# A list schedule's allowance for attention work on VectorE: fixed at 1.5, or 0.2 and 2.0 by the attention's share of the steps

## The chip, the cores and the metric

The kernel runs on one core of a Trainium2 chip. The time is the device time of one execution in microseconds (us). The profile is of one execution, taken by the hardware profiler. Engines: PE is TensorE's matmul row and PEld its weight loads, DVE is VectorE, ACT is ScalarE, POOL is GpSimd, SP is SyncE, which issues the DMAs.

## What is computed

The input x is 8 images of 56 x 56 places with 256 channels. Layer 0 is a group norm, a routed window attention with a depthwise 3 x 3 convolution, an output projection and a residual. Layer 1 takes the result as 3136 tokens per image: a layer norm, an attention over a window of 7 neighbours with a residual, then a layer norm and a recurrence over the tokens with a residual. In outline:

```python
# layer 0, for each of 49 regions of 64 places, 8 heads
score, index = top_k(q @ gathered_keys, 32)   # of 256 keys
out = softmax(score) @ v[index]
x = x + (out + conv3x3(v)) @ out_w + out_b
# layer 1
t = t + local_attention(layer_norm(t))        # 3 tokens to each side
# recurrence, batch 8, 3136 steps
i, o = sigmoid(x_t @ U + b + h @ V) ; g = tanh(...)
c = h * c + i * g
h = o * tanh(c)
t = t + hs
```

The recurrence is serial: each step needs the h of the step before it. The forget gate of the source is computed but not used, so three gates remain.

## The kernel before

The images are cut into 7 rows of 448 tokens. A unit is one row of one image; there are 56 units, row by row, the 8 images within a row. A unit takes queries and the convolution, then 7 regions. For each region, two pairs of head groups get scores from TensorE, and VectorE finds the top 32 of 256 by rounds of MAX8 and MATCH_REPLACE8 (each MATCH_REPLACE8 comes with a small MATCH_VALUE_LOAD). ScalarE takes exponentials, TensorE transposes and multiplies with the values. Behind a unit come its output projection, the local attention of layer 1 and the gates' input terms (tile gs), which go to DRAM (xgd) and are loaded again for the recurrence (r_gin). All of this is called attention here.

A step of the recurrence runs over four engines: 48 matmuls add h times the gate weights to the input terms (r_sum), ScalarE takes a tanh (r_th), VectorE transposes it (STREAM_TRANSPOSE r_cell<-r_th), VectorE scans to the new cell (TENSOR_TENSOR_SCAN r_c), ScalarE takes a second tanh (r_tc), and VectorE multiplies to the new h (SCALAR_TENSOR_TENSOR r_hs). This order is the chain. Beside it GpSimd prepares the next cell's product (r_cell<-r_hs,r_half). A row's steps can begin once that row is through attention in all 8 images. So the first steps stand beside the second row, and the last 451 steps can only follow the last attention. These last steps take the output gate's sum in a bank of its own, which leaves less on the chain.

The order of the instructions on each engine is made by the class _Plan. Every operation is first recorded with two estimates in ns: held, for which its engine is taken, and late, after which its result can be used (function _time). Operations of the recurrence's chain have chain set. _Plan.run then goes through time event by event. For each free engine it takes the first ready operation in order of rank, which is mostly the recurrence before attention, then the order of recording. An operation that isn't of the chain is held back if it would end after a bound called until. The function expected (line 414) gives due, the time at which the chain will next need the engine, by adding up late and a hop of 70 ns between engines. The bound is due plus an allowance. For the engines other than VectorE the allowance is a constant (SLACK, line 63: 60 for PE, ACT and POOL). For VectorE it is 1.5 times the time left until due, at least 20 (line 445). Where PE has nothing for more than 220 ns, a filler matmul on tile spare is put in (FILL). The estimates only make the order; on the chip each instruction waits for its semaphores. All recorded instructions have the helper's line 308 in the profile, the fillers line 661.

At the end of _layers, the loop over the units records attention and, at each row's second image, the steps whose row is complete (follow, line 1464). After the loop the remaining steps are recorded, and nc.run makes the order.

Of the kernel before, what the change touches and what calls it, by code (L numbers as in the profile page):

```python
# [56 lines left out]

HOP = 70
FAR = 10**12
FILL = 220  # L60
LONG = 400
CLEAR = 250
SLACK = {"PE": 60, "DVE": 120, "ACT": 60, "POOL": 60, "SP": 1000}
# [176 lines left out]
class _Plan:  # L240
# [137 lines left out]
    def run(self, tc, fill):  # L378
        ops = self.ops
        for tag in self.tags.values():  # L380
            for i, buf in enumerate(tag):
                kin = [b for b in tag[:i] if b.stream == buf.stream][-1:] if buf.free else tag[i - 1 : i]
                before = [(b.users[0], 0) for b in kin]
                if i >= buf.bufs and not buf.free:
                    before += [(u, None) for u in tag[i - buf.bufs].users]
                for u, gap in before:
                    for v in buf.users:
                        if u is not v:
                            g = gap
                            if g is None:  # L390
                                g = u.held if u.engine == v.engine else u.late + HOP
                            u.before[v] = max(g, u.before.get(v, 0))
        for op in ops:
            op.open, op.due = 0, 0
        for op in ops:
            for b in op.before:
                b.open += 1
        engines = ("PE", "DVE", "ACT", "POOL", "SP")
        free = dict.fromkeys(engines, 0)
        later = {e: [] for e in engines}  # L400
        ready = {e: [] for e in engines}
        chain = [o for o in ops if o.chain]
        at, made, events = 0, {}, []

        def opened(op):
            heappush(later[op.engine], (op.due, op.rank, op))
            heappush(events, op.due)

        for op in ops:
            if not op.open:  # L410
                opened(op)
        done, now = [], 0

        def expected(engine):


            t = None
            for k in range(at, min(at + 7, len(chain))):
                op = chain[k]
                if t is None:  # L420
                    if op.open:
                        break
                    t = max(op.due, now)
                else:
                    p = chain[k - 1]
                    t += p.late + (HOP if p.engine != op.engine else 30)
                if op.engine == engine or engine == "POOL" and op.pair:
                    return t - (CLEAR if engine == "POOL" else 0)
            return FAR

        filled = tied = 0
        locked = {"DVE": 0, "POOL": 0}
        since, closed = 0, None
        while len(done) < len(ops) + filled:
            moved = False
            for e in engines:
                if free[e] > now:
                    continue
                while later[e] and later[e][0][0] <= now:
                    _, rank, op = heappop(later[e])  # L440
                    insort(ready[e], (rank, op))
                if not ready[e]:
                    continue
                due = expected(e)
                until = due + (SLACK[e] if e != 'DVE' else max(20, 1.5 * (due - now)))
                for i, (rank, op) in enumerate(ready[e]):
                    if not op.chain and now + op.held > until:
                        continue
                    if op.pair and locked["POOL" if e == "DVE" else "DVE"] > now:
                        continue  # L450
                    if e == "POOL" and op.pair and op.held > LONG and 0 < at < len(chain):
                        if since > 3:
                            continue
                        op.behind = closed
                    if any(b.free and not self._room(b, made, now) for b in op.takes):
                        continue
                    del ready[e][i]
                    op.start = now
                    free[e] = now + op.held
                    if op.pair:  # L460
                        locked[e] = now + op.late
                        heappush(events, locked[e])
                    heappush(events, free[e])
                    heappush(events, now + op.late + HOP)
                    done.append(op)
                    for b in op.takes:
                        if b.free:
                            made.setdefault(id(b.tag), []).append(b)
                    for b, gap in op.before.items():
                        b.due = max(b.due, now + gap)  # L470
                        b.open -= 1
                        if not b.open:
                            opened(b)
                    if op.chain:
                        at += 1
                        since += 1
                        if op.closes:
                            since, closed = 0, op
                    elif e == "POOL" and op.rank[0] == 0:
                        tied += 1  # L480
                    moved = True
                    break
            if not moved and free["PE"] <= now:

                due = min([expected("PE")] + [op[0] for op in later["PE"][:1]])
                if FILL < due - now < FAR // 2:
                    op = _Op()
                    op.trace, op.start = [fill], now
                    filled += 1
                    done.append(op)  # L490
                    free["PE"] = now + FILL
                    heappush(events, free["PE"])
                    moved = True
            if not moved:
                while events and events[0] <= now:
                    heappop(events)
                if not events:
                    raise RuntimeError("the plan has stopped")
                now = heappop(events)
        self.length = now  # L500
        with tc.manual_schedule():
            for op in done:
                for t in op.trace:
                    t()
# [25 lines left out]
def _layers(ctx: ExitStack, tc, a, out):  # L530
# [9 lines left out]
    nc = tc.nc  # L540
# [7 lines left out]
    work = ctx.enter_context(tc.tile_pool(name="work", bufs=3))  # L548
# [89 lines left out]
    for t in cells:  # L638

        nc.vector.memset(t, 0.0)  # L640
        for at in (0, CELL + 2):
            e = t[:, at : at + CELL].rearrange("p (n e) -> p n e", e=3)
# [23 lines left out]
    raw, nc = nc, _Plan(tc)  # L666
    images_p, rowp, keep = nc.pool(images_p, nb), nc.pool(rowp, 2), nc.pool(keep, 2)
    one, work, two = nc.pool(one, 1), nc.pool(work, 3), nc.pool(two, 2)
# [789 lines left out]
    def after(g):  # L1458

        b, unit = units[g]  # L1460
        im, row = images[b], state_of[g]
        return project(b, unit, im, row) + window_attention(b, unit, im, row)

    def follow(first, end):

        with nc.rank(0):
            for k in range(first, end):
                for s in recurrence(k):
                    s()
# [26 lines left out]
            todo = todo[n:]  # L1496
    for s in after(len(units) - 1):
        s()
    made["tokens"] = SHIFTED
    follow(ready, -(-SHIFTED // TB))  # L1500
    nc.run(tc, fill)
# [2 lines left out]
def _body(tc, a, out):  # L1504
    _layers(tc, a, out)
# [64 lines left out]
```

## Time and profile before

| what | us |
|---|---|
| median of 3 runs | 9194.27 (9193.11 to 9199.71) |
| profiled execution, device time | 9180.4 |
| profiled execution, span from first to last instruction | 9178.5 |
| first scan of the recurrence starts | 1339.9 |
| last attention instruction on VectorE starts | 8032.4 |
| last scan starts | 9172.7 |

| engine | busy us | share of the span |
|---|---|---|
| PE | 8792.1 | 96% |
| PEld | 6037.0 | 66% |
| DVE | 7559.4 | 82% |
| ACT | 5939.4 | 65% |
| POOL | 3221.5 | 35% |

PE's share includes the fillers (14904 matmul records, 2072.2 us). The profile's rows of groups give busy time and mean duration of one instruction; instructions of one engine overlap, so that the distance from start to start is shorter than the duration. In the page's row of slices each digit is the busy share of a fortieth of the span, in tenths. A line of waits names who waited, for whom, us in total, times, and the longest. Where this text counts steps, it counts the scans, one per step (3136).

### The profile page before, as it was taken

Reading aid. Unit: us, or ns where it says so; the run is one execution under the profiler, and the core shown is the slowest. Engines: PE = TensorE matmul, PEld = TensorE weight load, DVE = VectorE, ACT = ScalarE, POOL = GpSimd, SP = SyncE. Lnnn points to the kernel's source line nnn. Section 1 sums busy time; section 2 is a strip of 40 time slices with the busy share of each in tenths; the row PEclk is TensorE's granted clock in tenths of the full one; section 3 lists DMA queues with packets and bytes.
Section 4 is the critical chain, followed back from the end, with each engine's and each line's share of the span. In section 5 each row is a group of like instructions: output and inputs, shape, how many; then the busy total and the mean of one; then the engine's idle time right before and its main releaser. Section 6 shows DMA issues by size and latency. Waiting matters only on the chain.

```text
span 9178.5 us, 500794 instructions
## 1 busy us (share of the span) xinstructions
PE 8792.1 (96%) x203918; PEld 6037.0 (66%) x203918; DVE 7559.4 (82%) x32392; ACT 5939.4 (65%) x23551; POOL 3221.5 (35%) x7747
## 2 busy tenths in 40 slices
PE   7999999999999999999999999999999999999999
PEld 4555556666666666666666666666666666688888
DVE  5776799999999899999899999899999999734443
ACT  4665667776666677676676676677766766534444
POOL 1232344444343343343344443434434444311111
PEclk9999999999999999999999999999999999999999
DMA  6545433333332333333333333233333232210000
GB/s 198 155 129 163 111 106 82 93 92 80 93 91 78 91 84 90 89 85 91 88 82 92 91 82 90 78 93 88 83 92 89 80 90 78 60 28 23 23 24 21
DMA packets 1071271, 798.40 MB, mean 87 GB/s; under 512 B 402366, under 2 KB 1001524, under 8 KB 1068964
## 3 DMA queue, kind: packets, MB, share of 16 engines
q1 hardware_dynamic: 1068964, 766.36, 30.8%
q8 instruction: 1604, 26.28, 1.2%
q14 instruction: 703, 5.76, 0.2%
HBM read 527.08 MB, written 238.88 MB: 83 GB/s over the span
## 4 chain that ended last, share of the span: by engine, by line
PE 52%; DVE 25%; ACT 6%; issue 2%; DMA 1%; SPq 0%; POOL 0%; ACTq 0%; DVEq 0%; POOLq 0%
PE r_sum L308 19%; PE mm L308 15%; PE spare L661 12%; DVE left L308 8%; DVE top L308 6%; DVE r_c L308 3%; PE pt_av L308 3%; PE sc L308 3%; DVE r_cell L308 2%; DVE r_hs L308 2%; ACT pe L308 1%; ACT r_th L308 1%; ACT xln L308 1%; DVE st L308 1%; ACT r_sum L308 1%
## 5 line engine op out<-in xcount | busy, mean ns | idle before, releaser
L308 PE MATMUL r_sum<-r_v,r_hs 128*16 128x64 f32 (+2 forms) x150528 | 2758.0, 220 | 160.4 <-DVE r_hs L308 107.1
L308 PEld LDWEIGHTS r_sum<-r_v,r_hs 128*8 128x8 f32 (+2 forms) x150528 | 2224.2, 96 | 907.8 <-DVE r_hs L308 802.6
L308 POOL TENSOR_TENSOR r_cell<-r_hs,r_half 128x16 f32<-128x16 f32 x3136 | 706.7, 225 | 4012.7 <-DVE r_hs L308 3192.8
L661 PE MATMUL spare<-ident 128*32 128x128 f32 x14904 | 2072.2, 276 | 6.2 <-issue 4.5
L308 DVE MATCH_REPLACE8 left<-top,left 128x256 f32<-128x256 f32 x4704 | 1903.3, 408 | 0.0
L308 DVE MAX8 top<-left 128x8 f32<-128x256 f32 x4704 | 1848.2, 413 | 1.8 <-POOL r_cell L308 0.3
L308 ACT ACTIVATE r_th<-r_sum 128x64 f32<-128x64 f32 x3587 | 802.3, 224 | 1559.4 <-PE r_sum L308 1507.1
L661 PEld LDWEIGHTS spare<-ident 128*32 128x32 f32 x14904 | 1474.8, 110 | 309.6 <-issue 263.4
L308 DVE STREAM_TRANSPOSE r_cell<-r_th 128x64 f32<-128x64 f32 x3136 | 812.8, 259 | 882.5 <-ACT r_th L308 842.2
L308 POOL TENSOR_TENSOR pe<-pe,left 128x256 f32<-128x256 f32 x1568 | 1136.2, 729 | 821.5 <-ACT left L308 397.9
L308 ACT ACTIVATE r_tc<-r_c 128x16 f32<-128x16 f32 x3136 | 696.9, 222 | 717.4 <-DVE r_c L308 696.0
L308 DVE TENSOR_TENSOR_SCAN r_c<-r_cell 128x48 f32<-128x48 f32 x3136 | 910.8, 290 | 86.9
L308 ACT ACTIVATE pe<-sc,nmax 128x256 f32<-128x256 f32 x1568 | 710.9, 470 | 185.5 <-DVE left L308 105.3
L308 ACT ACTIVATE left<-left,nmax 128x256 f32<-128x256 f32 x1568 | 773.8, 502 | 13.8 <-DVE left L308 7.8
L308 PE MATMUL pt_av<-ident,pe 128*128 128x128 f32 x3136 | 691.2, 289 | 49.4 <-ACT pts L308 19.4
L308 PE MATMUL mm<-wu,xlT 128*112 128x256 f32 (+3 forms) x1856 | 732.6, 512 | 2.6 <-ACT xlT L308 1.7
L308 DVE MAX8 top<-sc 128x8 f32<-128x256 f32 x1568 | 620.4, 416 | 80.8 <-PE sc L308 80.4
L308 ACT ACTIVATE r_half<-r_c 128x16 f32<-128x16 f32 x3136 | 655.3, 209 | 0.0
L308 DVE SCALAR_TENSOR_TENSOR r_hs<-r_cell,r_tc 128x16 f32<-128x16 f32 x2685 | 545.4, 203 | 124.5 <-ACT r_tc L308 103.4
L308 DVE MATCH_REPLACE8 left<-top,sc 128x256 f32<-128x256 f32 x1568 | 641.2, 412 | 0.7 <-issue 0.6
L308 ACT COPY pts<-pt_av 128x256 f32<-128x256 f32 x1568 | 574.8, 367 | 97.6 <-PE pt_av L308 89.5
L308 PEld LDWEIGHTS pt_av<-ident,pe 128*128 128x128 f32 x3136 | 375.3, 143 | 349.2 <-issue 190.0
(131 smaller groups left out, 12151.6 us busy)
## 6 DMA issues: line engine op xcount, KB each, us to landing
kg<-kd SPq DMA_DIRECT2D x1568, 64.0 KB
vg<-vd SPq DMA_DIRECT2D x1568, 64.0 KB
vshift<-lines SPq DMA_DIRECT2D x336, 232.0 KB
xgd<-gs SPq DMA_DIRECT2D x224, 336.0 KB
r_gin<-xgd SPq DMA_DIRECT2D x1568, 48.0 KB
xchunk<-xt SPq DMA_DIRECT2D x112, 448.0 KB
lines<-v SPq DMA_DIRECT2D x112, 290.0 KB
xn<-xh SPq DMA_DIRECT2D x56, 560.0 KB
```

Source lines behind the costliest of these rows:

```text
L308: made[:] = [method(*[v.real() if isinstance(v, _View) else v for v in args], **{k: v.real() if isinstance(v, _View) else v for k, v in kw ...
L661: raw.tensor.matmul(spare[:32, :P], ident[:, :32], ident, start=True, stop=True, skip_group_check=True)
```

## The change

The factor 1.5 for VectorE is replaced by a function, yields. It keeps account of spent, the estimated VectorE time (held) of all operations placed so far that are not of the chain. work is the sum of held over all such operations recorded before the last 451 steps (nc.last marks that place), and beside is the number of chain operations there. begun is what was spent when the first chain operation was placed, and at is the number of chain operations placed. Attention counts as ahead when what was spent since begun is more than the share at / beside, plus AHEAD = 0.02, of what was left at begun. Then the factor is 0.2; otherwise it is 2.0. Every other rule of the list stays.

```diff
+AHEAD = 0.02
...
+        beside = sum(o.chain for o in ops[:self.last])
+        work = sum(o.held for o in ops[:self.last] if o.engine == "DVE" and not o.chain)
+        begun = 0
+
+        def yields():
+
+            ahead = spent - begun - (at / beside + AHEAD) * (work - begun)
+            return 0.2 if ahead > 0 else 2.0
+
-        filled = tied = 0
+        filled = tied = spent = 0
...
-                until = due + (SLACK[e] if e != 'DVE' else max(20, 1.5 * (due - now)))
+                until = due + (SLACK[e] if e != "DVE" else max(20, yields() * (due - now)))
...
+                    if e == "DVE" and not op.chain:
+                        spent += op.held
                     if op.chain:
+                        begun = begun if at else spent
                         at += 1
...
+        self.spent = spent
...
+    nc.last = len(nc.ops)
     made["tokens"] = SHIFTED
     follow(ready, -(-SHIFTED // TB))
     nc.run(tc, fill)
```

## The prediction

> **What bounds the kernel now.** I read the page first, then busy time by stage, then the recurrence's scans counted by stage, then VectorE's waits and a stretch of its timeline.
>
> From the page:
>
> ```profile
> span 9178.5 us, 500794 instructions
> ...
> DVE  5776799999999899999899999899999999734443
> ...
> PEclk9999999999999999999999999999999999999999
> ...
> PE 52%; DVE 25%; ACT 6%; issue 2%; DMA 1%; SPq 0%; POOL 0%; ACTq 0%; DVEq 0%; POOLq 0%
> ```
>
> VectorE (DVE) is nearly full from slice 7 to slice 34, where attention runs beside the recurrence, and at 40% once the attention is done. TensorE's clock is full throughout. Busy time by stage (columns: length; busy time and instructions of PE, PEld, DVE, ACT, POOL; clock; DMA):
>
> ```profile
> 1340.00:4000.00 2660.00, 2568.42 (x65014) 1725.24 (x65011) 2466.90 (x10618) 1856.49 (x7484) 1074.22 (x2565) 1.00 0.33 88
> 4000.00:7700.00 3700.00, 3571.05 (x90567) 2387.54 (x90569) 3413.91 (x14693) 2574.66 (x10384) 1492.97 (x3581) 1.00 0.33 87
> ```
>
> The same for the instructions on tile r_c alone; VectorE's count there is the number of scans, one per step:
>
> ```profile
> 1340.00:7700.00 6360.00, 743.93 (x2471) 830.85 (x4942) 1.00 0.33 87
> ...
> 8032.00:8220.00 188.00, 22.21 (x83) 27.86 (x166) 1.00 0.11 29
> 8220.00:9178.00 958.00, 106.26 (x449) 150.34 (x899) 1.00 0.08 23
> ```
>
> This decides the reading. A step takes 6360/2471 = 2.574 us beside attention, 188/83 = 2.265 us in the same form once VectorE has no attention left (its last such instruction starts at 8032.4), and 958/449 = 2.13 us in the late form that splits off the output gate. VectorE carries about five attention operations, near 1.7 us by their start distances, in a step that is only 0.31 us longer for them. So **the chain of the recurrence sets the time, not the amount of VectorE work**: the attention ends early, and 451 late steps follow whatever happens. What counts is by how much each attention operation delays the chain.
>
> I then split the 2.574 us by the starts in the trace (means over the first 2560 steps, against the usual value where nothing interferes): scan to second tanh 0.376 (0.293), that tanh to the h product 0.271 (0.256), product to first matmul 0.325 (0.235), first tanh to transpose 0.314 (0.256), transpose to scan 0.296 (0.296). VectorE's own share is the last two and the second: 148 us from a late transpose, 39 us from a late product, nothing between transpose and scan. ScalarE and TensorE cost more. VectorE's waits over 1340 to 7700 agree: it waits for the chain in only 350 of 2470 transposes, otherwise it comes to it from attention work.
>
> ```profile
> DVE r_cell L308 <- ACT r_th L308: 241.5, 350, 3.6
> DVE r_hs L308 <- ACT r_tc L308: 69.2, 216, 3.0
> ```
>
> VectorE's timeline (start, duration, instruction):
>
> ```profile
> 3108.29 0.41 DVE L308 MAX8 top<-left 128x8 f32<-128x256 f32 x1
> 3108.63 0.40 DVE L308 BATCH_NORM_STATS2 st<-t 112x6 f32<-112x256 f32 x1
> ...
> 3111.70 0.27 DVE L308 STREAM_TRANSPOSE r_cell<-r_th 128x64 f32<-128x64 f32 x1
> 3111.87 0.25 DVE L308 SCALAR_TENSOR_TENSOR r_res<-mm,r_res 128x128 f32<-128x128 f32 x1
> 3112.05 0.24 DVE L308 TENSOR_TENSOR_SCAN r_c<-r_cell 128x48 f32<-128x48 f32 x1
> ...
> 3114.15 0.26 DVE L308 STREAM_TRANSPOSE r_cell<-r_th 128x64 f32<-128x64 f32 x1
> 3114.45 0.26 DVE L308 TENSOR_TENSOR_SCAN r_c<-r_cell 128x48 f32<-128x48 f32 x1
> ```
>
> Independent instructions overlap: what follows a MAX8 starts 0.34 us after it (median 0.341), though it is busy for 0.41; what follows the transpose starts 0.165 to 0.17 after it. The scan needs the transpose's result and starts 0.296 after it (last two lines). So between the two there is room for about 0.13 us of other work; the r_res operation there already puts the scan at 0.345.
>
> **The change, part by part.** It adds no instruction, DMA or tile. It replaces the factor 1.5 in VectorE's test by 0.2 or 2.0, depending on whether attention is ahead of its share plus 2%. What this does to the list I take from the two built orders of VectorE, counted up to the last match_replace (2565 steps before the change, 2624 after it), by the three gaps that a step has.
>
> *Transpose to scan.* The code's estimates: the transpose holds VectorE for 166 ns, its scan is due at 276, so 110 remain; a MAX8 is put at 326. Factor 1.5 allows 110 + 165 = 275, factor 2.0 allows 110 + 220 = 330. So at 2.0, and not at 1.5, a whole MAX8 passes in front of the scan. The orders show it: operations of 0.33 us and more in this gap go from 0 to 798 (789 of them MAX8). No row of before has one there. By the start distances the scan moves from 0.296 to 0.165 + 0.341 = 0.506, so +0.210 us each: 798 x 0.210 = **+168 us**. Bounds: 0 if other engines are late anyway; without overlap 0.258 + 0.413 - 0.296 = 0.375 each, 299 us. I take 0.210, built from the nearest rows, and correct for other engines below. Against that, operations of about 0.2 us there go from 133 to 57, at 0.05 each: -4 us.
>
> The Trainium skill, page "VectorE: DVE Perf Modes", section "The DRAIN you can't avoid", says that the next operation does not start until the pipe is empty (and that one that is not held starts earlier). Read strictly, that is the 299 us; the rows above show the overlap, so I go by them.
>
> *Product to next transpose.* With factor 0.2 a fourth long operation is mostly refused. I added up the start distances of the operations in this gap (MAX8 0.341, match load plus match_replace 0.399, others likewise), and took the mean from first tanh to transpose in before for each sum:
>
> - under 1.1 us: 0.256, 203 steps before, 479 after
> - 1.1 to 1.3: 0.267, 373 and 1096
> - 1.3 to 1.4: 0.284, 219 and 218
> - 1.4 to 1.5: 0.317, 1411 and 660
> - 1.5 and more: 0.401, 359 and 171
>
> The excess over 0.256 adds up to 148 us before and 83 us after: **-65 us**. Here the lower factor pays, since it also takes work from steps where the transpose was late.
>
> *Scan to product.* One long operation passes under all three factors (373 ns are left, a match_replace is put at 391). The same kind of table gives 39 us before and 40 after: +1.
>
> *What lies beside it.* A later scan or transpose lets TensorE finish what it had begun: from product to first matmul takes 0.335 after a punctual transpose, 0.311 after one that is 0.14 late, 0.287 after one that is 0.25 late. So about a fifth comes back. ScalarE gives nothing back: scan to tanh is 0.368 after punctual and after late transposes alike. The gates' supply stays covered: the last gate copy of row 5 moves from step 2168 to 2223, and its first use is at 2237, 14 steps or 36 us later.
>
> *Sum.* 168 - 4 - 65 + 1 = 100, times 0.8 = **+80 us**. That the attention ends 59 steps later costs and brings nothing by itself: the work on ScalarE and TensorE that disturbs the chain is the same, spread more thinly. 9180.4 (the profiled execution) + 80 = 9260; the median of the runs shown is 13.9 above that execution, so 9274. A hint from the orders alone: TensorE's fillers, placed where the list leaves it idle, grow by 594 beside attention and fall by 411 behind it.
>
> **Rivals.**
>
> 1. VectorE's throughput is the bound (the side opposite to mine, faster). For it: VectorE is busy 5880.8 of 6360 us from 1340 to 7700. Then 59 more steps beside attention cost only their own start distances, 0.165 + 0.175 + 0.093 = 0.433 us each, +26, and 59 steps fewer behind it save 2.265 each, -134: -108 us, median 9086. It decides as soon as the step beside attention, whose mean was 2.574, does not lengthen when a MAX8 stands before the scan. Against it: steps with three, four and five operations ahead of the transpose took nearly the same in before (2.55, 2.59, 2.59).
>
> The Trainium skill, page "Perfetto Trace Analysis", section "Identifying the Most-Contended Engine", would take the engine with the highest occupancy as the bound, which by the stage table is VectorE, and would arrive at this rival's sum; the 2.265 us of a step with an empty VectorE speaks against it.
>
> 2. Other engines hide the new delay. ScalarE and TensorE hold up the chain by 0.083 and 0.090 us a step on average. If the 0.210 swallowed 60% of its price, 168 x 0.4 = 67 against -69: no change, 9194. The fifth measured above speaks against it.
>
> 3. The supply runs dry at row boundaries: 14 steps instead of 69 at the last. If POOL or the DMA queue needed more than 36 us there, each of the five boundaries would add its excess; ten us each is +50 on top, 9324.
>
> **How the numbers follow.** About 0.2% (18 us) is what a measurement of this kernel can tell from no change. My forecast with its spread, slower by 10 to 150 us, has 0.73; rival 3 has 0.04; rival 2 has 0.12, most of it within 0.2%; rival 1 and lesser gains have 0.11. The range goes down to 9170, so that it takes in rival 2, and up to 9350: the bound without overlap would give 299 - 68 = +231, and two thirds of that is +154, 9348 on the median's scale. Faster 0.13, within 0.2% 0.11, slower 0.76.
>
> **What would show it.** After the change: some 800 steps in which a MAX8 stands between transpose and scan, with the scan about 0.5 us after the transpose; a longer mean step beside attention, about 2.60 us; the last attention instruction at about step 2660 instead of 2604; steps behind it unchanged at 2.13. If those 800 scans come late and the mean step is still no longer, rival 2 is right. If the mean step falls below 2.55, my reading of the bound is wrong.

## The result, and the profile after

The changed kernel takes 9245.48 us (median of 5 runs, 9235.69 to 9268.9) against 9194.27 us. The ratio is 1.0053, with a 95% interval from 1.0042 to 1.0065: slower by 49 us (39 to 60). The profiled execution took 9235.7 us, 55 more than that of before.

From the page of the changed kernel:

```profile
span 9234.0 us, 501605 instructions
...
DVE  5676799998898989998998999889898888854443
...
PEclk9999999999999999999999999999999999999999
...
PE 61%; DVE 15%; ACT 7%; issue 2%; DMA 1%; SPq 0%; POOL 0%; ACTq 0%; POOLq 0%; DVEq 0%
```

VectorE's attention reaches further (slices 35 and 36 stand at 8 and 5, in before at 7 and 3), and more of the slices ahead of them stand at 8 instead of 9. VectorE's share of the chain that ended last falls from 25% to 15%, although the kernel is slower. Scans by stage, the count of DVE being the steps:

```profile
1348.00:7700.00 6352.00, 707.47 (x2459) 828.10 (x4917) 1.00 0.32 85
7700.00:8209.00 509.00, 52.94 (x198) 67.18 (x398) 1.00 0.29 76
...
8275.00:9234.00 959.00, 106.59 (x450) 150.50 (x900) 1.00 0.09 23
```

A step beside attention takes 6352/2459 = 2.583 us (2.574 before): longer, but by 0.009 us and not by the 0.026 of the forecast sign (2.60). The last attention instruction on VectorE starts behind 2657 steps (2604 before), and the late steps keep their 959/450 = 2.13 us. VectorE's waits from 1348 to 7700:

```profile
DVE r_cell L309 <- ACT r_th L309: 422.1, 928, 3.9
DVE r_hs L309 <- ACT r_tc L309: 60.6, 188, 1.6
```

It now stands ready for the transpose in 928 steps instead of 350: the factor 0.2 does what it says. What the factor 2.0 does shows in VectorE's timeline:

```profile
5102.88 0.26 DVE L309 STREAM_TRANSPOSE r_cell<-r_th 128x64 f32<-128x64 f32 x1
5103.05 0.39 DVE L309 MAX8 top<-left 128x8 f32<-128x256 f32 x1
5103.35 0.23 DVE L309 TENSOR_TENSOR_SCAN r_c<-r_cell 128x48 f32<-128x48 f32 x1
...
5105.45 0.26 DVE L309 STREAM_TRANSPOSE r_cell<-r_th 128x64 f32<-128x64 f32 x1 [0.26 <-ACT r_th L309]
5105.75 0.26 DVE L309 TENSOR_TENSOR_SCAN r_c<-r_cell 128x48 f32<-128x48 f32 x1
...
5107.78 0.27 DVE L309 STREAM_TRANSPOSE r_cell<-r_th 128x64 f32<-128x64 f32 x1 [0.16 <-ACT r_th L309]
5107.95 0.39 DVE L309 MAX8 top<-sc 128x8 f32<-128x256 f32 x1
5108.27 0.23 DVE L309 TENSOR_TENSOR_SCAN r_c<-r_cell 128x48 f32<-128x48 f32 x1
```

In the first and third step a MAX8 stands between transpose and scan, and the scan starts 0.47 and 0.49 us after the transpose; in the second it starts after 0.30. In the whole trace 780 steps have a MAX8 there and 10 a BATCH_NORM_STATS2, with a median of 0.475.

To see where the time went, I added up each link of the chain, start to start, over the first 2560 steps of the profiled executions, in us against before:

| link | changed | extra MAX8 | 0.2 and 1.5 | fixed 2.0 |
|---|---|---|---|---|
| transpose to scan | +143.5 | +157.0 | +2.1 | +252.3 |
| first tanh to transpose | -68.1 | +29.4 | -19.6 | +2.7 |
| second tanh to product | +9.1 | +4.0 | +3.6 | +21.0 |
| scan to second tanh | -62.4 | -50.8 | -23.2 | -57.3 |
| product to first matmul | +24.3 | -48.2 | +19.5 | +30.7 |
| the 48 matmuls | -6.1 | -21.6 | -3.5 | -7.6 |
| last matmul to first tanh | -8.6 | +1.5 | -6.8 | -24.2 |
| sum | +31.7 | +71.3 | -27.9 | +217.7 |

(The other columns are experiments below.) Each column compares one execution with one. Executions of before alone lie up to 27 us apart (9178.76 to 9205.32 in one series), and the profiled one, 9180.4, is one of the fastest. So a link that differs by less than about 10 us says little, and a sum can miss the timed difference by up to 24 us (fixed 2.0: spans 226 apart, timed 202).

For the changed kernel, the steps from 2560 to 2685 add 16.3, since attention stands beside more of them, the first scan starts 8.5 later, and the late steps take 1.1 less: 55.4 in all, the difference of the spans. The 8.5 isn't clearly the change's: the extra-MAX8 kernel, whose list is that of before, starts 6.9 later in its profile.

### The profile page after: what moved, and what is told of

Same layout as the page of the kernel before. It is cut to its first block, busy times and chain, and to the rows that moved or that the text cites. A ratio compares the mean times of both kernels' runs of the same rounds, so it can differ in the third digit from the quotient of the medians.

```text
span 9234.0 us, 501605 instructions
## 1 busy us (share of the span) xinstructions
PE 8841.5 (96%) x204284; PEld 6075.4 (66%) x204284; DVE 7491.2 (81%) x32392; ACT 5941.0 (64%) x23551; POOL 3219.6 (35%) x7747
## 4 chain that ended last, share of the span: by engine, by line
PE 61%; DVE 15%; ACT 7%; issue 2%; DMA 1%; SPq 0%; POOL 0%; ACTq 0%; POOLq 0%; DVEq 0%
PE r_sum L309 22%; PE mm L309 18%; PE spare L675 12%; DVE left L309 4%; PE pt_av L309 4%; PE sc L309 4%; DVE top L309 3%; DVE r_c L309 2%; DVE r_cell L309 2%; DVE r_hs L309 2%; ACT r_th L309 1%; ACT pe L309 1%; ACT xln L309 1%; ACT left L309 0%; ACT et L309 0%
## 5 line engine op out<-in xcount | busy, mean ns | idle before, releaser
L675 PE MATMUL spare<-ident 128*32 128x128 f32 x15270 | 2111.9, 276 | 7.4 <-issue 5.7
L675 PEld LDWEIGHTS spare<-ident 128*32 128x32 f32 x15270 | 1517.1, 110 | 308.8 <-issue 255.5
L309 DVE TENSOR_TENSOR_SCAN r_c<-r_cell 128x48 f32<-128x48 f32 x3136 | 875.0, 279 | 64.8
L309 PE MATMUL mm<-wu,xlT 128*112 128x256 f32 (+2 forms) x1856 | 734.4, 512 | 3.3 <-ACT xlT L309 2.5
```

What stands on the lines that cost most here:

```text
L309: made[:] = [method(*[v.real() if isinstance(v, _View) else v for v in args], **{k: v.real() if isinstance(v, _View) else v for k, v in kw ...
L675: raw.tensor.matmul(spare[:32, :P], ident[:, :32], ident, start=True, stop=True, skip_group_check=True)
```

## The experiments

The theory: the recurrence's chain sets the time, and the loss is the MAX8 that the factor 2.0 lets in between transpose and scan. Rival 1: VectorE's throughput is the bound. Rival 2: other engines hide VectorE's delays.

**The price of one MAX8 in that place, in the order of before.**

```diff
+    scrap = const.tile([P, 8], F32, name="scrap")
...
                     nc.vector.transpose(gates, blocks(th))
+                    if at % 3 == 0:
+                        nc.ops[-1].trace.append(lambda: raw.vector.max(scrap, wo[:, 0, :]))
```

> The order of before, with one MAX8 over 256 columns of a constant into a scratch tile issued between transpose and scan in every third step of those beside attention (895 steps); the list doesn't know of it. Main theory (the chain of the recurrence sets the time, and a MAX8 in front of the scan puts the scan from 0.296 to 0.475 us after the transpose, as the trace of the changed kernel shows): 895 x 0.179 = 160 us at most, 95 if other engines give back 40%: ratio 1.010 to 1.0175. Rival 1 (VectorE's throughput is the bound): 895 x 0.31 to 0.34, +280 to +305, ratio 1.030 or more. Rival 2 (other engines hide the delay): under +35, ratio below 1.004.

Measured: ratio 1.0079 (1.0066 to 1.0093), +72 us, or 0.081 for each MAX8. The trace's group of them:

```profile
L1372 DVE MAX8 scrap<-wo x895: 373/384/390, 1346.5 to 8293.5; 128x8 f32<-128x256 f32 x179
```

895 instructions of 0.384 us are 344 us. VectorE's busy time grows by only 146 of them (7559.4 to 7705.0 by the pages), because each MAX8 overlaps with its neighbours and fills part of the gap that stood empty between transpose and scan. So the 280 us that the text above gives rival 1 are too many: as VectorE's own sequence gets longer by 0.179 each, rival 1 too would lose 160. The kernel loses 72, which lies between the theory's range (95 to 160) and rival 2's (under 35).

In the steps that have the MAX8, the scan to second tanh falls from 0.379 to 0.329, product to first matmul from 0.315 to 0.265, and the matmuls (to the end of the last) from 0.896 to 0.880; in the other steps these links move by 0.005 or less. So ScalarE and TensorE give back 121 us of the scans' 157, most of it in just the steps that were held up. It fits that what they had begun for the attention is finished by the time the chain comes. Another 29 us are lost ahead of the transpose, nearly all in the other steps (0.314 to 0.330 on average), to which VectorE comes later. Taken together, about half of the delay stays.

**Less work on VectorE, in the order of before.**

```diff
-                    nc.vector.max(top[g2][:, r, :], src[g2])
+                    nc.vector.max(top[g2][:, r, :], src[g2][:, :64] if r == ROUNDS - 1 else src[g2])
+                    nc.timed(326, 416)
```

> The order of before, but the MAX8 of the last of the four rounds reads 64 of the 256 columns (so this round looks at a quarter of the scores): 1568 instructions shorter by about 192 columns, some 0.2 us each, 310 us less work on VectorE, all of it beside or ahead of the recurrence. Main theory (the chain): only late transposes and products gain, from 148 + 39 us of excess perhaps a third to a half: -40 to -90 us, ratio 0.990 to 0.996. Rival 1 (VectorE's throughput): about -250 to -310 us, ratio 0.966 to 0.973. Rival 2 (other engines cover VectorE's delays): 0 to -40, ratio 0.996 to 1.0.

Measured: 0.9985 (0.9976 to 0.9994), -14 us, below the main theory's range and within rival 2's. The groups of this kernel (count, busy us, mean ns, idle before and its releaser):

```profile
L308 DVE STREAM_TRANSPOSE r_cell<-r_th 128x64 f32<-128x64 f32 x3136 | 818.3, 261 | 1024.3 <-ACT r_th L308 984.3
```

```profile
L308 DVE MAX8 top<-left 128x8 f32<-128x64 f32 x1568 | 302.1, 214 | 1.2 <-POOL r_cell L308 0.7
```

and the first of them in before:

```profile
L308 DVE STREAM_TRANSPOSE r_cell<-r_th 128x64 f32<-128x64 f32 x3136 | 812.8, 259 | 882.5 <-ACT r_th L308 842.2
```

This kernel leaves three quarters of the scores out of the last round; the order and the number of instructions are those of before. 1568 MAX8 of 0.214 instead of 0.413 us are 312 us less, and VectorE's busy time falls by 250 (7559.4 to 7309.4 by the pages; the rest is overlap). VectorE's wait for the first tanh ahead of the transpose grows by 142 us, and the kernel gains 14. The profiled execution, 9194.2, is one of the slower of its kernel, so this trace doesn't show in which link the 14 lie. That is the end of rival 1, which asked for 250 to 310.

**The factor 1.5 in place of 2.0.**

```diff
-            return 0.2 if ahead > 0 else 2.0
+            return 0.2 if ahead > 0 else 1.5
```

> The changed kernel with the factors 0.2 and 1.5 instead of 0.2 and 2.0: by the built order no long operation stands between transpose and scan, and the attention ends at step 2629, as late as in the changed kernel. Main theory: the loss is gone, and the table of late transposes (121 us against 148) leaves -15 to -30 us against before, ratio 0.9967 to 0.9985. Rival 1 (VectorE's throughput, so that what counts is how much attention is left beside the steps): -100 us, ratio 0.989. A third reading, that the loss comes from the later end of the attention or from the factor 0.2 and not from the MAX8 in the gap: +40 to +50 as in the changed kernel, ratio 1.004 to 1.0055.

Measured: 0.9979 (0.9970 to 0.9988), -19 us, as the theory has it. Attention ends as late as in the changed kernel, and the toggle is there: neither of them costs. The table above shows transpose to scan back at that of before.

**Only the gap closed again.** The changed kernel, but with less than 150 ns left the factor is 0.2; the last 451 steps are as they were.

```diff
-                until = due + (SLACK[e] if e != "DVE" else max(20, yields() * (due - now)))
+                until = due + (SLACK[e] if e != "DVE" else max(20, (yields() if due - now > 150 or at >= beside else 0.2) * (due - now)))
```

> The changed kernel with one thing taken back: where less than 150 ns are left until the chain needs VectorE (that is, above all, between transpose and scan) the factor is 0.2, everywhere else 0.2 or 2.0 as in the change; the last 451 steps keep their order. By the built order no long operation stands in that gap, attention ends at step 2627 (2624 in the changed kernel), late-transpose excess 142 us by the table (148 in before, 83 in the changed kernel). Main theory: the change's +49 us go, since they are the MAX8 in this gap: -15 to +5 against before, ratio 0.998 to 1.0005. If the loss comes from the factor 2.0 elsewhere, from the toggle or from the later end of the attention: +30 to +50, ratio 1.003 to 1.0055. Rival 1 (VectorE's throughput): -100, ratio 0.989.

Measured: 1.0007 (0.9998 to 1.0016), +6 us, one more than the theory's range. Of the change's 49 us, 43 go with this one gap. That is a balance: in this kernel's trace transpose to scan is at -7.8 against before instead of +143.5, but the gain from first tanh to transpose is gone too (-4.1 instead of -68.1), as the expected 142 us of late transposes had it.

**Attention as far ahead as in before.** AHEAD = 0.04.

> The changed kernel with AHEAD 0.04 instead of 0.02: by the built order the attention ends at step 2569, as in before, and 897 long operations stand between transpose and scan. Main theory: 897 x 0.179 = 161 us, less some 53 us of late transposes, less what other engines give back: +55 to +108, ratio 1.006 to 1.012, more than the changed kernel's 1.0053. Rival 1, and the reading that the later end of the attention is the loss: VectorE has the same work beside the same steps as in before, so 0, ratio 0.998 to 1.002.

Measured: 1.0062 (1.0048 to 1.0076), +57 us, within the theory's range, and far from the 0 of an account by VectorE's work or by the end of attention. Its interval overlaps that of the changed kernel, so that the hundred more MAX8 aren't shown by the time alone. In the trace 872 MAX8 stand in the gap.

**A fixed factor of 2.0.** The kernel of before with 2.0 for 1.5.

> The kernel of before with the fixed factor 2.0 instead of 1.5: by the built order 1382 long operations between transpose and scan (none before), the late-transpose excess 135 us by the table (148), attention's end at step 2444 (2565). Main theory with the share that stays by the runs so far (0.081 of each 0.179): 1382 x 0.081 = 112, -7 for the transposes: +90 to +130 us, ratio 1.010 to 1.014; at the full price +235, ratio 1.026. Rival 1 (VectorE's throughput): 121 fewer steps beside attention, -52, and 121 more behind it, +274: +220, ratio 1.024.

Measured: 1.0220 (1.0206 to 1.0234), +202 us: I had expected too little. The time alone would also fit rival 1, which the shorter MAX8 excludes. 1354 scans come late here. By the table ScalarE gives back 57 us, much as with 895 or 780 MAX8, and TensorE gives back nothing. So the share that stays, 0.45 where the list doesn't know of the MAX8, isn't a constant: in the three lists that plan for them (changed, AHEAD 0.04, fixed 2.0) product to first matmul grows by 24 to 31 us instead of shrinking by 48. Part of this isn't the MAX8's: the list with 0.2 and 1.5, which has none there, is at +19.5. The rest fits what the traces hold on TensorE between the chain's last matmul and the first of the next step. In the changed kernel these are on average 13.4 matmuls of the attention in steps with a MAX8 in the gap and 11.1 in the others, with the fixed factor 2.0 13.9 and 10.2. With the extra MAX8, which the list doesn't know, they are 11.8, as in the same steps of before. So a list that plans for the MAX8 fills the longer step with more matmuls; that these hold up the next step is likely, but no run separates it.

**The same MAX8 where no attention is left.** In each of the last 451 steps, in no other.

```diff
+    scrap = const.tile([P, 8], F32, name="scrap")
...
                     nc.vector.transpose(gates, blocks(th))
+                    nc.ops[-1].trace.append(lambda: raw.vector.max(scrap, wo[:, 0, :]))
                 with nc.rank(-1):
```

> The order of before, with the extra MAX8 into a scratch tile between transpose and scan in each of the 451 last steps, where no attention is left, and in none beside attention. Beside attention 895 such MAX8 cost 72 us, 0.081 each, though each moved its scan by 0.175. If other engines gave back the rest because attention work of their own stood in the chain's way there, here nothing can give back: 451 x 0.179 = 81 us, +70 to +90, ratio 1.0076 to 1.010. If a MAX8 in this place simply costs 0.08 to the chain: +36 us, ratio 1.004. If VectorE's work sets the time (rival 1): 0, since VectorE is 40% busy there.

Measured: 1.0059 (1.0046 to 1.0073), +54 us, between the two expectations; in the trace this stage takes 57.9 us more. VectorE's timeline of two such steps:

```profile
8700.24 0.26 DVE L308 STREAM_TRANSPOSE r_cell<-r_th 128x64 f32<-128x64 f32 x1 [1.01 <-ACT r_th L308]
8700.41 0.39 DVE L1383 MAX8 scrap<-wo 128x8 f32<-128x256 f32 x1
...
8700.71 0.24 DVE L308 TENSOR_TENSOR_SCAN r_c<-r_cell 128x48 f32<-128x48 f32 x1
...
8702.42 0.26 DVE L308 STREAM_TRANSPOSE r_cell<-r_th 128x64 f32<-128x64 f32 x1 [0.81 <-ACT r_th L308]
8702.59 0.39 DVE L1383 MAX8 scrap<-wo 128x8 f32<-128x256 f32 x1
8702.90 0.22 DVE L308 STREAM_TRANSPOSE r_tr<-r_th 128x64 f32<-128x64 f32 x1
8703.05 0.22 DVE L308 TENSOR_TENSOR_SCAN r_c<-r_cell 128x48 f32<-128x48 f32 x1
```

The scan is moved by 0.172 on average. Without attention, too, something can give back: in every second step ScalarE has a second r_th and a copy of terms to do before the second tanh, and scan to second tanh falls from 0.361 to 0.270 in these and not in the others. 0.172 less half of 0.091 (half, as it is every second step) is 0.127, times 451 is 57. VectorE is 40% busy here, and pays all the same.

The second of these steps shows something else: the list puts the transpose of the output gate (r_tr) in front of the scan.

**A fixed factor of 0.8.** The kernel of before with 0.8 for 1.5.

> The kernel of before with the fixed factor 0.8 instead of 1.5: by the built order no long operation between transpose and scan, excess by the tables 153 us from late transposes (of it some 14 from one step in which the list waits for the next row) and 15 from late products (148 and 44), attention's end at step 2647. Main theory, half of the difference of 32 us stays: -10 to -25 us, ratio 0.9973 to 0.999. A reading that the toggle itself, and not the room between transpose and scan, matters: no gain, ratio 0.999 to 1.002. Rival 1: 82 more steps beside attention, -150 us.

Measured: 0.9971 (0.9959 to 0.9983), -27 us: two more than expected, and for another reason. From the first scan to scan 2685 its trace takes 6887.2 us (6877.4 in before), so nothing is gained there on balance; from there to the last scan it takes 929.5 instead of 955.4. With factor 0.8 no late step has r_tr in front of the scan (226 have it in before). The table of late transposes hadn't looked there.

Nor had it looked at the row boundaries. With this factor the attention comes so late that the recurrence has to wait for it, as at the last boundary (the rs2o is the last of the attention on VectorE):

```profile
8203.17 0.26 DVE L308 TENSOR_TENSOR_SCAN r_c<-r_cell 128x48 f32<-128x48 f32 x1
...
8211.25 0.17 DVE L308 SCALAR_TENSOR_TENSOR rs2o<-mv,rs 112x5 f32<-112x5 f32 x1 [1.65 <-POOL rs L308]
8230.51 0.27 DVE L308 STREAM_TRANSPOSE r_cell<-r_th 128x64 f32<-128x64 f32 x1 [19.10 <-ACT r_th L308]
8230.82 0.26 DVE L308 TENSOR_TENSOR_SCAN r_c<-r_cell 128x48 f32<-128x48 f32 x1
```

These two scans are 27.65 us apart, 2.03 in before. The six steps at row boundaries take 71.9 us together, in before 14.7; the other steps up to scan 2685 take 47 less than in before. So the smaller factor gains beside attention and loses it again at the boundaries.

**Smaller factors, and AHEAD 0.01.**

```diff
-AHEAD = 0.02
+AHEAD = 0.01
...
-            return 0.2 if ahead > 0 else 2.0
+            return 0.6 if ahead > 0 else 1.2
```

> The changed kernel with the factors 0.6 and 1.2 and AHEAD 0.01: by the built order nothing long between transpose and scan, excess by the tables 128 us from late transposes and 24 from late products (148 and 44 in before, 121 and 44 with 0.2 and 1.5), attention's end at step 2646. Main theory, half of the 40 us stays: -20 to -35 us against before, ratio 0.9962 to 0.998, at least as fast as 0.2 and 1.5. If only the end of the attention counted (rival 1): -150 us.

Measured: 0.9979 (0.9970 to 0.9988), -19 us, at the edge of the expectation and no better than 0.2 and 1.5: the tables' further 13 us, of which half was to stay, don't show. Here, too, the recurrence stands still at the last boundary: the scan after it comes 13.33 us behind the one before it (2.03 in before).

**What the others pointed to.** Factors 0.2 and 1.5, and 0.2 in the last 451 steps.

```diff
-            return 0.2 if ahead > 0 else 2.0
+            return 0.2 if ahead > 0 or at >= beside else 1.5
```

> The factors 0.2 and 1.5 as before, and 0.2 in the last 451 steps: there the factor 1.5 or 2.0 lets the transpose of the output gate pass in front of the scan in every second step (223 of 445 by the built order), with 0.2 in none. In the traces such a step has its scan 0.453 us after the transpose instead of 0.298; the kernel with the fixed factor 0.8, which has none of them, takes 929.5 us from scan 2685 to the last instead of 955.4. Main theory (what stands in front of the scan is paid by the chain): 26 us on top of the 20 of 0.2 and 1.5: -40 to -52 against before, ratio 0.9945 to 0.9957. If other work hides it in timed runs: -20, ratio 0.998.

Measured: 0.9954 (0.9940 to 0.9967), -42 us, faster than both kernels. A late step of before with r_tr in front, then one of this kernel:

```profile
8703.17 0.26 DVE L308 STREAM_TRANSPOSE r_cell<-r_th 128x64 f32<-128x64 f32 x1 [1.01 <-ACT r_th L308]
8703.45 0.24 DVE L308 STREAM_TRANSPOSE r_tr<-r_th 128x64 f32<-128x64 f32 x1
8703.62 0.21 DVE L308 TENSOR_TENSOR_SCAN r_c<-r_cell 128x48 f32<-128x48 f32 x1
```

```profile
8700.48 0.26 DVE L309 STREAM_TRANSPOSE r_cell<-r_th 128x64 f32<-128x64 f32 x1 [1.01 <-ACT r_th L309]
8700.78 0.26 DVE L309 TENSOR_TENSOR_SCAN r_c<-r_cell 128x48 f32<-128x48 f32 x1
8700.96 0.22 DVE L309 STREAM_TRANSPOSE r_tr<-r_th 128x64 f32<-128x64 f32 x1
```

The scan follows its transpose after 0.30 instead of 0.45. Scans counted from 8300 to 9100, in before and in this kernel:

```profile
8300.00:9100.00 800.00, 89.22 (x377) 126.14 (x754) 1.00 0.08 23
```

```profile
8300.00:9100.00 800.00, 99.73 (x388) 129.84 (x776) 1.00 0.09 24
```

11 steps more in the same 800 us: 2.062 instead of 2.122 a step. From scan 2685 to the last scan it is 26 us (955.4 to 929.3).

## Why the prediction was right, and where its sizes were off

- **The bound** was read rightly. 250 us less busy time on VectorE gain 14. MAX8 added in front of the scan cost 72, though no engine but VectorE got more work. The prediction didn't weigh TensorE, whose matmul row is busier than VectorE in its stage table (2568.42 of 2660 us). Of TensorE's 6139 us there from 1340 to 7700, fillers take 1043; no run changes TensorE's work alone.
- **Transpose to scan**, the term that decided: predicted 168 - 4, measured +143.5 over the first 2560 steps. Of these the 764 long operations there make 136.5, and the other steps +7.0 where I had -4. The count was right (798 in the order, 790 in the whole trace). The price was put at 0.210 and is 0.179, because the scan starts 0.306 after a MAX8, where in before the next instruction, whatever it is, starts 0.341 after one. I had no row of a scan behind a MAX8 and took the distance to whatever came next. That is 798 x 0.031 = 25 us, and 20 of the 31 by which I was too high once the factor 0.8 of my sum is applied.
- **Product to next transpose**: -65 predicted, -68 measured. The table of before, read with the counts of the new order, held.
- **Scan to product**: +1 predicted, +9 measured.
- **What other engines give back** was wrong in its mechanism: predicted were 20 on TensorE and nothing on ScalarE. The trace has it the other way round: ScalarE -62, TensorE's links and the tanh behind them +10 together. My sentence that ScalarE gives nothing back was drawn from late transposes; a late scan is another thing, since ScalarE can do work of its own between the first tanh and the second. The extra-MAX8 kernel shows the effect directly, 0.379 to 0.329 in just those steps. In size, 53 came back over these 2560 steps, but not all for the late scans: with 0.2 and 1.5, where no MAX8 stands in the gap, the same links give back 14, since the attention is spread over more steps, and in the changed kernel the steps from 2560 to 2685, which now stand beside attention, take 16 more. So some 37 to 39 stand against my 20.
- **The later end of attention** was to cost nothing by itself. The kernel with 0.2 and 1.5, in which it is as late, confirms that: its trace gains 28 us in the first 2560 steps and loses 19 in the 125 behind them. On balance 9 are gained, where VectorE's own links give 14; the traces can't tell these two apart.
- **Sum**: +80 predicted, +49 measured (39 to 60), +55 in the profile. Against that 55 I was too high by 31 on the MAX8 (before anything is given back), by 16 on the other engines and by 3 on the transposes; 11 on short operations in the gap, 8 on the products, and 7 on the start and the late steps went the other way. That these offset each other in part is chance. The direction doesn't hang on it.
- **Rivals**: throughput (1) fell with the shorter MAX8, and with the kernel with AHEAD 0.04, where it asked for no change. Hiding (2) is half true: in the order of before 55% of the price is hidden (72 of 160 us stay), which is near the 60% at which it would have decided; in the changed kernel it is about a quarter (37 to 39 of 143.5). A dry supply (3) didn't come here: the six steps at row boundaries take 2.03 to 3.16 us, and the longest stretch of 112 steps, at the start of the recurrence, 2.74 us a step. It came with the fixed factor 0.8.

What stays open: TensorE gives back 70 us when the MAX8 are unknown to the list, and nothing when it plans for them. The matmuls counted above fit this, but no run changes TensorE's order alone.

## What to carry to other kernels

Where a serial chain shares an engine with filler work, ask of each gap in the chain what an operation there costs, not how full the engine is. Here a MAX8 ahead of the transpose often falls into time that the chain spends elsewhere, and the same MAX8 between two chain operations on one engine puts the second off by 0.18 us. An allowance in proportion to the time left misses this: at 2.0 it let a whole MAX8 into a gap with room for 0.13 us. Too small an allowance has a price as well, as the 27.65 us at a row boundary show. A count of the built order, priced by distances from start to start in the old trace, told the direction and the place before the run; its weak terms were the price of a pair of instructions that the old trace didn't have, and what other engines give back.

## What the runs showed of the hardware that was not expected

- A scan behind a MAX8 starts 0.306 us after it (median of the changed kernel's trace), though in before the next instruction starts 0.341 after one.
- 895 MAX8 of 0.384 us between transpose and scan raised VectorE's busy time by 0.163 us each, not by 0.384: they overlap with both neighbours.
- VectorE's share of the chain that ended last fell from 25% to 15% while VectorE's own place in the loss grew. That view follows at each step what ended last, and this share didn't tell where the loss was.
- 250 us of busy time taken from an engine that was 92% busy beside the recurrence gave 14 us.
